# Self-attention softmax of a decoder layer: begun one batch ahead, with row sums and division on VectorE

## The chip, the cores and the metric

One core of a Trainium2 chip runs the whole layer in one launch. The metric is the device time of one execution in microseconds (us), the median of several executions. Engines are called as in the profile: PE (TensorE's matrix products, with PEld for its weight loads), DVE (VectorE), ACT (ScalarE), POOL (GpSimd) and SP, whose queue issues most DMAs.

## The reference, cut to what matters

A decoder layer in fp32 for 16 batches of 112 tokens with 512 features: self-attention with 16 heads of 32, cross-attention to 375 context tokens, and a gated feed-forward block, each behind a layer norm. The change is in the self-attention's softmax:

```python
scores = jnp.einsum('bhqr,bhkr->bhqk', q_r, k_r) * scale     # scale = 1/sqrt(32)
attn = jax.nn.softmax(scores, axis=-1)
y_r = jnp.einsum('bhqk,bhkr->bhqr', attn, v_r)
```

## The kernel before, in words

Tokens are taken in four groups of four batches. For a group, `Group.queries`, `keys` and `values` project the normalised tokens (`xyT`, features on partitions) into `q`, `k` and one `v` per batch. Self-attention then goes batch by batch, by the calls `lay(0)` to `lay(15)` (L1629 to L1672); each call is called a step here.

A step has a fixed order on PE. `scores` (L902) makes, for all 16 heads, 112 x 112 scores with the queries on partitions, in two PSUM tiles of the tag `sc` (two tiles exist, eight heads in each). VectorE takes each row's maximum (L1005) and subtracts it (L1007); ScalarE takes the exponential (L1010) of eight heads in one operation. PE transposes each head's block (L1024) back into the `sc` tiles, so that the keys come onto the partitions, and ScalarE copies that to SBUF as `eT` (L1026). `weighted_values` (L915) multiplies with `v` into the PSUM tile `ys`, and `key_sums` (L930) multiplies the same `eT` with a block of ones, which puts the softmax's row sums into a PSUM bank of the tag `mm`. `Pending` keeps both; its `store`, called in the next step, divides: four reciprocals (L952) and one multiplication (L953) that writes the result into `xyT`.

Between these pieces PE does other work, so that it need not wait. `Filler` holds a queue of such pieces (projections of later groups, products that prepare the feed-forward weight `w2`, transposes of normalised tokens, the output projection `after_self`, first products of cross-attention). A step's second argument `us` says how much of it is to be spread over the step: at least 5.5 us between the scores and the first transposes, further shares after each half's transposes, and `f.drain()` emits what is left at the end. These pieces write into PSUM banks of the tag `mm`, of which three exist; most are emptied by a ScalarE copy (L857, L871, L888, L1538, L827), the output projection by VectorE (L990) and the first cross-attention values by VectorE (L888).

PE's order is the program's order (`manual_schedule`). The other engines' orders are laid out by the framework's planner, which knows estimated costs and takes earlier lines first among what is ready; on the chip each engine then works its queue in that order. `tc.issue_after(x)` puts a block's instructions behind `x` on the engine of `x`. That is used for `pending.store()` and for the preparation of `w2` (`w2_prep`, a generator whose steps are two or three VectorE operations, a ScalarE copy L1567 or some stores by DMA); a step's `prepared` says how many are taken.

SBUF tiles: `pair(name, tag, bufs)` gives a tile for eight heads, and `evp` also holds the cross-attention queries under the tag `q`, which have the same size.

Of the kernel before, what the change touches and what calls it, by code (L numbers as in the profile page):

```python
# [11 lines left out]
F32 = mybir.dt.float32  # L12
I32 = mybir.dt.int32
U8 = mybir.dt.uint8
AF = mybir.ActivationFunctionType
ALU = mybir.AluOpType
AX = mybir.AxisListType

P = 128
B, S, D = 16, 112, 512  # L20
# [3 lines left out]
C = D // P  # L24
H, DH = 16, 32
HG = 4
# [4 lines left out]
GB = 4  # L31
# [4 lines left out]
SCALE = 1.0 / math.sqrt(DH)  # L36
# [548 lines left out]
def mixed(a, b, skip=0):  # L585

    a, b = iter(a), iter(b)
    for _ in range(skip):
        yield next(a)
    while True:  # L590
        took = [next(p, None) for p in (a, b)]
        if took[0] is None and took[1] is None:
            return
        yield sum(t for t in took if t is not None)
# [3 lines left out]
def finite_layer(  # L598
# [30 lines left out]
    nc = tc.nc  # L629
# [12 lines left out]
    def psum(tag, shape, bufs=None):  # L642
        bufs = bufs or banks_of.get(tag, 2)
        return ps[""].tile(shape, F32, tag=tag, bufs=bufs, name=tag)
# [7 lines left out]
    def pair(name, tag="e", bufs=3):  # L652
        return evp.tile([P, 2, HG, S], F32, tag=tag, name=name, bufs=bufs)
# [148 lines left out]
    class Norm:  # L802


        def __init__(self, l, tiles):
            self.l, self.tiles = l, tiles
# [10 lines left out]
        def begin(self):  # L817
            self.start(True)
            yield 0.0
# [18 lines left out]
    def block_products(k):  # L838
        tr = psum("mm", [P, C, P])
        nc.tensor.transpose(tr[:, 0, :], bd[k], ident)  # L840
        nc.scalar.copy(bd[k], tr[:, 0, :])
        nc.tensor.matmul(tr[:, 1, :], bd[0], bd[k], start=True, stop=True)
        nc.scalar.copy(bdm[k], tr[:, 1, :])
        yield 0.5

    def fold(dst, src, block):

        for m in range(C):
            acc = psum("mm", [P, D])
            for j in range(C):  # L850
                if block is None:
                    nc.tensor.transpose(acc[:, ts(j, P)], src[:, j, ts(m, P)], ident)
                else:
                    nc.tensor.matmul(
                        acc[:, ts(j, P)], src[:, j, ts(m, P)], block, start=True, stop=True
                    )
            nc.scalar.copy(dst[:, m, :], acc)  # L857
            yield 0.9
# [43 lines left out]
    def scores(k_of, q_of, rows_):  # L902

        scs = [psum("sc", [P, 2, 512]) for _ in range(2)]
        views = [
            s[:rows_, :, : HG * S].rearrange("p i (j s) -> p i j s", j=HG) for s in scs
        ]
        for j in range(C):
            for i in range(HG):
                nc.tensor.matmul(  # L910
                    views[i // 2][:, i % 2, j, :], k_of(i, j), q_of(i, j), start=True, stop=True
                )
        return views

    def weighted_values(y, v, es, first, last):  # L915


        n = v.shape[0]
        for j in range(C):
            for i in range(HG):  # L920
                nc.tensor.matmul(  # L921
                    y[ts(i, DH), j, :],
                    v[:, HG * j + i, :],
                    es[i // 2][:n, i % 2, j, :],
                    start=first and j == 0,
                    stop=last,
                    skip_group_check=True,
                )

    def key_sums(sums, es, n):  # L930
        for i in range(HG):
            nc.tensor.matmul(  # L932
                sums[ts(i, DH), :, :], ones[:n, :DH], es[i // 2][:n, i % 2], start=True, stop=True
            )

    class Pending:


        def __init__(self):
            self.kept = None  # L940

        def put(self, *kept):
            self.kept = kept

        def store(self):
            if self.kept is None:
                return
            y, sums, b, scale, over = self.kept
            self.kept = None
            r = ln.tile([P, C, S], F32, tag="r", name="r")  # L950
            for c in range(C):
                nc.vector.reciprocal(r[:, c], sums[:, c])  # L952
            nc.vector.scalar_tensor_tensor(  # L953
                xyT[:, :, ts(b, S)], in0=y, scalar=scale, in1=r, op0=ALU.mult, op1=ALU.mult
            )
            if over is not None:
                nc.scalar.activation(
                    r, r, AF.Relu, scale=-1.0, bias=limit[:, 1:], accum_out=over
                )

    pending = Pending()


    class Group:

# [26 lines left out]
            stats(xr[:, t, :], norm.l, t)  # L992
        norm.start(False)

    def self_attention(b, grp, f, us, prepared):
        bl = b % GB
        scs = scores(
            lambda i, j: grp.q[ds(i * DH, DH), j, ts(bl, S)],
            lambda i, j: grp.k[ds(i * DH, DH), j, ts(bl, S)],
            S,  # L1000
        )
        es = []
        for sc in scs:
            mx = ln.tile([S, 2, HG], F32, tag="mx", name="mx")
            nc.vector.reduce_max(mx, sc, axis=AX.X)  # L1005
            e = pair("e", "es", 3)[:S]
            behind = nc.vector.tensor_tensor(  # L1007
                e, sc, mx.unsqueeze(3).to_broadcast([S, 2, HG, S]), ALU.subtract
            )
            nc.scalar.activation(e, e, AF.Exp, scale=SCALE)  # L1010
            es.append(e)
        with tc.issue_after(behind.ins):
            pending.store()
            for _ in range(prepared):
                next(w2_prep, None)
        first = max(0.45 * us, min(us, 5.5))
        f.fill(first)
        eTs = []
        for e, share in zip(es, (0.45 * (us - first), 0.35 * (us - first))):
            tr = psum("sc", [P, 2, 512])  # L1020
            trv = tr[:S, :, : HG * S].rearrange("p i (j s) -> p i j s", j=HG)
            for i in range(2):
                for j in range(C):
                    nc.tensor.transpose(trv[:, i, j, :], e[:, i, j, :], ident[:S, :S])  # L1024
            eT = pair("eT")
            nc.scalar.copy(eT[:S], trv)  # L1026
            eTs.append(eT)
            f.fill(share)
        y = psum("ys", [P, C, S])
        sums = psum("mm", [P, C, S])  # L1030
        weighted_values(y, grp.v[bl][:S], eTs, True, True)
        key_sums(sums, eTs, S)
        pending.put(y, sums, b, 1.0, None)
        f.drain()

# [194 lines left out]
    class Cross:  # L1232
# [6 lines left out]
        def step(self, b, kc, q, keys, f, us):  # L1239
            scs = scores(  # L1240
                lambda i, j: keys.k[ds(i * DH, DH), j, ts(kc, KP)],
                lambda i, j: q[ds(i * DH, DH), j, ts(b % 2, S)],
                KP,
            )
            n = b * KC + kc
            late = self.late

            es = [(pair("es", "es", 3) if kc == 0 else pair("e"))[:KP] for _ in scs]
            self.late = (b, kc, keys.v[kc][:KP], es)
            for i, sc in enumerate(scs):  # L1250
                nc.scalar.activation(  # L1251
                    es[i], sc, AF.Exp, scale=scl[:, n : n + 1], bias=bia[:, n : n + 1]
                )
            for i, sc in enumerate(scs):
                nc.scalar.activation(  # L1255
                    sc,
                    sc,
                    AF.Relu,
                    scale=nscl[:, n : n + 1],
                    bias=limit[:KP, :1],  # L1260
                    accum_out=low[:KP, 2 * n + i : 2 * n + i + 1],
                )
            self.weigh(late)
            for i in range(2):
                self.add(late, i)
            self.divide(late)
            f.fill(us)
# [15 lines left out]
        def divide(self, late):  # L1283
            if late is not None and late[1] == KC - 1:
                sums = psum("mm", [P, C, S])
                key_sums(sums, self.es, KP)

                pending.put(
                    self.y, sums, late[0], 1.0 / (1.0 + 1e-8), top[:, late[0] : late[0] + 1]
                )  # L1290
                pending.store()

# [303 lines left out]
    f = Filler()  # L1598
# [15 lines left out]
    f.drain()  # L1614
    n1[1].start(True)
    f.add(mixed(grp[0].keys(), block_products(1)))
    f.add(mixed(fold(wv, raws[2], bdm[1]), n1[1].transposes()), grp[0].values(range(GB)))
    f.drain()
    w2_load()
# [4 lines left out]

    def lay(b, us, *pieces, prepared=0):
        f.add(*pieces)
        self_attention(b, grp[b // GB], f, us, prepared)

    lay(0, 15.5, mixed(grp[1].queries(), w2_products(h, w2[0])))  # L1629
    lay(1, 15.5, mixed(grp[1].keys(), w2_products(h, w2[1])), prepared=4)  # L1630
# [39 lines left out]
    lay(14, 12, mixed(kv[0].values(), n2[2].transposes(), 3))  # L1670
    qs = [Queries(n) for n in range(B // 2)]
    lay(15, 9.5, qs[0].pieces(), output_bias())  # L1672
    pending.store()

    cross = Cross()
    n3w = None
# [1 line left out]
    for b in range(B):  # L1678
        g, bl = divmod(b, GB)
        us = 0.0  # L1680
# [183 lines left out]
```

## Time and profile before

| | |
|---|---|
| median of three runs | 1392.72 us (1392.26 to 1393.63) |
| profiled execution, its own time | 1394.03 us |
| span of that execution, first to last instruction | 1392.2 us |
| PE busy | 1364.3 us (98%) |
| VectorE, ScalarE, GpSimd busy | 794.7, 428.8, 33.9 us |
| granted TensorE clock | 0.997 |
| steps 0 to 15 of self-attention | 63.4 to 341.6 us |
| cross-attention, then feed-forward | 341.6 to about 853 us, then to the end |

Such lines are read as follows. A group of instructions has its line, engine, operation, the tiles it writes and reads, its shape and count, then total busy time and the mean of one in ns, then the engine's idle time just before it and what ended that. The timeline has start and length in us, the same names, and in brackets the idle time before. A line of waits says which engine and line waited for which, in total, how often, and the longest. fp32 products stand in the trace as two records each. A busy PE is not a PE at its peak, since products are pipelined; costs on PE are therefore better read from start to start.

### The profile page before, as it was taken

Reading aid. Unit: us, or ns where it says so; the run is one execution under the profiler, and the core shown is the slowest. Engines: PE = TensorE matmul, PEld = TensorE weight load, DVE = VectorE, ACT = ScalarE, POOL = GpSimd, SP = SyncE. Lnnn points to the kernel's source line nnn. Section 1 sums busy time; section 2 is a strip of 40 time slices with the busy share of each in tenths; the row PEclk is TensorE's granted clock in tenths of the full one; section 3 lists DMA queues with packets and bytes.
Section 4 is the critical chain, followed back from the end, with each engine's and each line's share of the span. In section 5 each row is a group of like instructions: output and inputs, shape, how many; then the busy total and the mean of one; then the engine's idle time right before and its main releaser. Section 6 shows DMA issues by size and latency. Waiting matters only on the chain.

```text
span 1392.2 us, 20015 instructions
## 1 busy us (share of the span) xinstructions
PE 1364.3 (98%) x8456; PEld 810.2 (58%) x8456; DVE 794.7 (57%) x1477; ACT 428.8 (31%) x677; POOL 33.9 (2%) x68
## 2 busy tenths in 40 slices
PE   8999999999999999999999999999999999999997
PEld 6555555555676667766777775544555555555554
DVE  5146987776555575558454566756754235554332
ACT  3345352324254434443454455110110011111000
POOL 2000010110000100000000000000000000000000
PEclk9999999999999999999999999999999999999999
DMA  9100002601000000000000102111131122312201
GB/s 318 47 1 26 6 16 77 251 7 45 23 23 23 31 23 23 24 23 24 23 23 23 45 12 60 46 46 46 31 123 60 46 64 77 91 61 73 108 0 56
DMA packets 59719, 74.03 MB, mean 53 GB/s; under 512 B 2640, under 2 KB 47712, under 8 KB 57316
## 3 DMA queue, kind: packets, MB, share of 16 engines
q1 hardware_dynamic: 57952, 69.44, 15.1%
q0 software_dynamic: 672, 1.62, 0.4%
q8 instruction: 69, 1.13, 0.3%
q10 hardware_dynamic: 996, 1.59, 0.3%
q14 instruction: 30, 0.25, 0.1%
HBM read 61.63 MB, written 11.01 MB: 52 GB/s over the span
## 4 chain that ended last, share of the span: by engine, by line
PE 88%; DVE 6%; ACT 2%; DMA 1%; issue 1%; POOL 0%; SPq 0%; DVEq 0%; ACTq 0%; POOLq 0%
PE mm L883 14%; PE gate L1450 12%; PE mm L865 9%; PE mm L1103 9%; PE ys L1450 7%; PE mm L894 6%; PE gate L1384 6%; PE mm L1450 5%; PE sc L910 4%; PE ys L1384 3%; PE ys L921 3%; PE mm L1384 3%; PE sc L1024 2%; PE mm L932 2%; PE mm L826 1%
## 5 line engine op out<-in xcount | busy, mean ns | idle before, releaser
L883 PE MATMUL mm<-xv,cT 128*125 128x512 f32 x384 | 179.4, 603 | 3.3 <-DVE v L888 3.3
L1251 ACT ACTIVATE e<-sc,bia,scl 125x896 f32<-125x896 f32 x64 | 68.4, 1094 | 201.0 <-PE sc L910 201.0
L952 DVE RECIPROCAL r<-mm 128x112 f32<-128x112 f32 x128 | 95.5, 808 | 42.5 <-PE mm L932 42.5
L883 PEld LDWEIGHTS mm<-xv,cT 128*125 128x125 f32 x384 | 68.4, 187 | 79.1 <-issue 74.1
L1255 ACT ACTIVATE sc<-sc,limit,nscl 125x896 f32<-125x896 f32 x96 | 102.6, 1068 | 0.0
L1450 PE MATMUL gate<-t,f 128*128 128x448 f32 x256 | 101.4, 539 | 0.0
L1281 DVE TENSOR_TENSOR es<-es,e 125x896 f32<-125x896 f32 x64 | 68.4, 1088 | 47.3 <-ACT e L1251 47.3
L1384 PE MATMUL gate<-h,f 128*128 128x448 f32 x224 | 86.6, 539 | 0.0
L1450 PE MATMUL gate<-xyT,f 128*128 128x448 f32 x192 | 80.1, 540 | 0.0
L1005 DVE TENSOR_REDUCE mx<-sc 112x8 f32<-112x896 f32 x32 | 33.5, 1082 | 77.1 <-PE sc L910 77.1
L1450 PE MATMUL ys<-t,f 128*128 128x448 f32 x192 | 77.4, 539 | 0.0
L1450 PEld LDWEIGHTS gate<-t,f 128*128 128x128 f32 x256 | 48.6, 190 | 47.6 <-issue 47.0
L1103 PEld LDWEIGHTS mm<-kt,xks 128*128 128x128 f32 x360 | 59.0, 190 | 15.3 <-issue 14.6
L1384 PEld LDWEIGHTS gate<-h,f 128*128 128x128 f32 x224 | 42.5, 190 | 41.3 <-issue 40.9
L1466 ACT COPY u<-gate 128x448 f32<-128x448 f32 x16 | 8.5, 531 | 182.3 <-PE gate L1450 109.4
L1103 PE MATMUL mm<-kt,xks 128*128 128x188 f32 x360 | 63.5, 324 | 0.0
L883 PE MATMUL mm<-wv,xyT 128*112 128x512 f32 x128 | 57.8, 596 | 0.3 <-ACT v L888 0.3
L1450 PEld LDWEIGHTS ys<-t,f 128*128 128x128 f32 x192 | 36.5, 190 | 35.7 <-issue 35.5
L865 PE MATMUL mm<-xyT,xq 128*128 128x224 f32 x256 | 52.5, 356 | 4.2 <-ACT xyT L827 4.0
L1396 DVE TENSOR_TENSOR h<-h,h 128x896 f32<-128x896 f32 x32 | 32.8, 1086 | 40.9 <-PE ys L1384 31.6
L1450 PEld LDWEIGHTS gate<-xyT,f 128*128 128x128 f32 x192 | 36.0, 190 | 34.4 <-issue 33.7
L910 PE MATMUL sc<-q,kT 32*125 32x112 f32 x1536 | 54.7, 279 | 0.0
(209 smaller groups left out, 2148.0 us busy)
## 6 DMA issues: line engine op xcount, KB each, us to landing
f<-in_f_w SPq DMA_DIRECT2D x64, 256.0 KB, 3.2
f<-blocks SPq DMA_DIRECT2D x14, 1024.0 KB, 4.8
cT<-in_ctx SPq DMA_DIRECT2D x16, 750.0 KB, 4.7
w<-in_f_w SPq DMA_DIRECT2D x4, 1024.0 KB, 10.5
blocks<-w SPq DMA_DIRECT2D x4, 1024.0 KB, 5.4
xr<-in_x SPq DMA_DIRECT2D x2, 1024.0 KB, 10.7
out_y<-o SPq DMA_DIRECT2D x8, 256.0 KB, 3.2
xr<-in_x SPq DMA_DIRECT2D x2, 768.0 KB, 15.4
```

The lines of the kernel that those rows point to most:

```text
L865: nc.tensor.matmul(acc[:, :n], w[:, c, ts(j, P)], src[:, c, :], start=(c == 0), stop=(c == C - 1))
L883: nc.tensor.matmul(acc[:n, :], src[:, c, :], w[:, c, :], start=(c == 0), stop=(c == C - 1))
L894: nc.tensor.matmul(acc, xyT[:, c, ts(t, P)], w[:, c, :], start=(c == 0), stop=(c == C - 1))
L910: nc.tensor.matmul(views[i // 2][:, i % 2, j, :], k_of(i, j), q_of(i, j), start=True, stop=True)
L921: nc.tensor.matmul(y[ts(i, DH), j, :], v[:, HG * j + i, :], es[i // 2][:n, i % 2, j, :], start=first and j == 0, stop=last, skip_group_che ...
L952: nc.vector.reciprocal(r[:, c], sums[:, c])
L1103: nc.tensor.matmul(acc[:, m], lhs[:, k, ts(m, P)], rhs[:, k], start=first and m == 0 and k == 0, stop=k == 1, skip_group_check=True,)
L1251: nc.scalar.activation(es[i], sc, AF.Exp, scale=scl[:, n : n + 1], bias=bia[:, n : n + 1])
L1255: nc.scalar.activation(sc, sc, AF.Relu, scale=nscl[:, n : n + 1], bias=limit[:KP, :1], accum_out=low[:KP, 2 * n + i : 2 * n + i + 1],)
L1281: nc.vector.tensor_tensor(total, total, late[3][i][:KP], ALU.add)
L1384: nc.tensor.matmul(banks[m][bank], o[:, c, ts(m, P)], t[:, c, :], start=first and c == 0, stop=c == UNITS - 1, skip_group_check=True,)
L1450: nc.tensor.matmul(bank, o[:, s, k, :], t[:, k, :], start=first and k == 0, stop=k == 1, skip_group_check=True,)
```

## The change

`self_attention` becomes a class with two methods. `begin(b)` makes the scores of a batch and the whole softmax: VectorE takes the maxima and multiplies them by -1/sqrt(32); ScalarE takes the exponential straight from PSUM, head by head, with that column as its bias (16 operations of 112 columns for each batch in place of two of 896); VectorE sums the rows, inverts the sums and multiplies. `step(b)` first begins batch b + 1 and then goes on with the transposes of batch b, whose values are divided already. The product with ones goes, and `y` is copied into `xyT` by ScalarE at the end of the same step. The first half's exponentials now lie in a tile of the tag `q`, of which two exist. `begin(0)` comes before step 0, after `grp[0].keys()`, with a `drain` ahead of it. The preparation of `w2` is issued behind the last multiplication of the begun batch, where it was behind the last subtraction. Cross-attention keeps its product with ones and its division, whose lines now stand in `Cross.divide`.

```diff
-    def self_attention(b, grp, f, us, prepared):
...
-        for sc in scs:
-            mx = ln.tile([S, 2, HG], F32, tag="mx", name="mx")
-            nc.vector.reduce_max(mx, sc, axis=AX.X)
-            e = pair("e", "es", 3)[:S]
-            behind = nc.vector.tensor_tensor(
-                e, sc, mx.unsqueeze(3).to_broadcast([S, 2, HG, S]), ALU.subtract
-            )
-            nc.scalar.activation(e, e, AF.Exp, scale=SCALE)
-            es.append(e)
-        with tc.issue_after(behind.ins):
-            pending.store()
...
-        y = psum("ys", [P, C, S])
-        sums = psum("mm", [P, C, S])
-        weighted_values(y, grp.v[bl][:S], eTs, True, True)
-        key_sums(sums, eTs, S)
-        pending.put(y, sums, b, 1.0, None)
+    class SelfAttention:
+        def begin(self, b, grp):
...
+            for sc, (tag, bufs) in zip(scs, (("q", 2), ("es", 3))):
+                mx = ln.tile([S, 2, HG], F32, tag="mx", name="mx")
+                nc.vector.reduce_max(mx, sc, axis=AX.X)
+                nc.vector.tensor_scalar(mx, mx, -SCALE, None, op0=ALU.mult)
+                e = pair("e", tag, bufs)[:S]
+                for i in range(2):
+                    for j in range(HG):
+                        nc.scalar.activation(
+                            e[:, i, j, :],
+                            sc[:, i, j, :],
+                            AF.Exp,
+                            scale=SCALE,
+                            bias=mx[:, i, j : j + 1],
+                        )
+                es.append((e, mx))
+            for e, total in es:
+                nc.vector.reduce_sum(total, e, axis=AX.X)
+                nc.vector.reciprocal(total, total)
+                self.behind = nc.vector.tensor_tensor(
+                    e, e, total.unsqueeze(3).to_broadcast([S, 2, HG, S]), ALU.mult
+                )
+            self.next = b, grp.v, [e for e, _ in es]
+
+        def step(self, b, grp, f, us, prepared):
+            b, v, es = self.next
+            if b + 1 < B:
+                self.begin(b + 1, grp)
+            with tc.issue_after(self.behind.ins):
+                for _ in range(prepared):
+                    next(w2_prep, None)
...
+            y = psum("ys", [P, C, S])
+            weighted_values(y, v[b % GB][:S], eTs, True, True)
+            nc.scalar.copy(xyT[:, :, ts(b, S)], y)
+            f.drain()
...
     f.add(mixed(grp[0].keys(), block_products(1)))
+    f.drain()
+    attention = SelfAttention()
+    attention.begin(0, grp[0])
     f.add(mixed(fold(wv, raws[2], bdm[1]), n1[1].transposes()), grp[0].values(range(GB)))
...
-        self_attention(b, grp[b // GB], f, us, prepared)
+        attention.step(b, grp[min(b + 1, B - 1) // GB], f, us, prepared)
```

More of the change, by code (lines that the diff above doesn't have):

```diff
@@ L934, in key_sums @@
             )
[L936 to L954, printed above, removed]
-            )
[L956 to L961, printed above, removed]
     class Group:
@@ L993, in after_self @@
         norm.start(False)
-    def self_attention(b, grp, f, us, prepared):
[L996 to L1002, printed above, removed]
-        for sc in scs:
-            mx = ln.tile([S, 2, HG], F32, tag="mx", name="mx")
-            nc.vector.reduce_max(mx, sc, axis=AX.X)
-            e = pair("e", "es", 3)[:S]
-            behind = nc.vector.tensor_tensor(
-                e, sc, mx.unsqueeze(3).to_broadcast([S, 2, HG, S]), ALU.subtract
-            )
-            nc.scalar.activation(e, e, AF.Exp, scale=SCALE)
-            es.append(e)
-        with tc.issue_after(behind.ins):
-            pending.store()
[L1014 to L1028, printed above, removed]
-        y = psum("ys", [P, C, S])
-        sums = psum("mm", [P, C, S])
-        weighted_values(y, grp.v[bl][:S], eTs, True, True)
-        key_sums(sums, eTs, S)
-        pending.put(y, sums, b, 1.0, None)
-        f.drain()
@@ new lines, in finite_layer @@
+    class SelfAttention:
+        def begin(self, b, grp):
+            bl = b % GB
+            scs = scores(
+                lambda i, j: grp.q[ds(i * DH, DH), j, ts(bl, S)],
+                lambda i, j: grp.k[ds(i * DH, DH), j, ts(bl, S)],
+                S,
+            )
+            es = []
+            for sc, (tag, bufs) in zip(scs, (("q", 2), ("es", 3))):
[27 more added lines that the diff above has]
+                    next(w2_prep, None)
+            first = max(0.45 * us, min(us, 5.5))
+            f.fill(first)
+            eTs = []
+            for e, share in zip(es, (0.45 * (us - first), 0.35 * (us - first))):
+                tr = psum("sc", [P, 2, 512])
+                trv = tr[:S, :, : HG * S].rearrange("p i (j s) -> p i j s", j=HG)
+                for i in range(2):
+                    for j in range(C):
+                        nc.tensor.transpose(trv[:, i, j, :], e[:, i, j, :], ident[:S, :S])
+                eT = pair("eT")
+                nc.scalar.copy(eT[:S], trv)
+                eTs.append(eT)
+                f.fill(share)
+            y = psum("ys", [P, C, S])
+            weighted_values(y, v[b % GB][:S], eTs, True, True)
+            nc.scalar.copy(xyT[:, :, ts(b, S)], y)
+            f.drain()
@@ L1286, in divide @@
                 key_sums(sums, self.es, KP)
-                pending.put(
-                    self.y, sums, late[0], 1.0 / (1.0 + 1e-8), top[:, late[0] : late[0] + 1]
-                )
-                pending.store()
+                b = late[0]
+                r = ln.tile([P, C, S], F32, tag="r", name="r")
+                for c in range(C):
+                    nc.vector.reciprocal(r[:, c], sums[:, c])
+                nc.vector.scalar_tensor_tensor(
+                    xyT[:, :, ts(b, S)],
+                    in0=self.y,
+                    scalar=1.0 / (1.0 + 1e-8),
+                    in1=r,
+                    op0=ALU.mult,
+                    op1=ALU.mult,
+                )
+                nc.scalar.activation(
+                    r, r, AF.Relu, scale=-1.0, bias=limit[:, 1:], accum_out=top[:, b : b + 1]
+                )
     UNITS = FC // 2
@@ L1672, in finite_layer @@
     lay(15, 9.5, qs[0].pieces(), output_bias())
-    pending.store()
     cross = Cross()
```

## The prediction

> **What bounds the kernel now.** I read the page's busy shares and chain first, then the step windows, the PE waits, and the timeline of single steps. "Step b" is `lay(b)`.
>
> ```profile
> PE 1364.3 (98%) x8456; PEld 810.2 (58%) x8456; DVE 794.7 (57%) x1477; ACT 428.8 (31%) x677; POOL 33.9 (2%) x68
> ...
> PE 88%; DVE 6%; ACT 2%; DMA 1%; issue 1%; POOL 0%; SPq 0%; DVEq 0%; ACTq 0%; POOLq 0%
> ```
>
> TensorE carries the end: any matmul removed is time removed, and every PE wait counts in full, because PE has no idle time in which to catch up. ScalarE and VectorE have room on average; what matters is how late they hand PSUM banks back.
>
> ```profile
> PE sc L1024 <- ACT e L1010: 2.8, 3, 1.4
> PE mm L865 <- ACT kT L871: 0.8, 1, 0.8
> PE ys L921 <- ACT eT L1026: 0.7, 1, 0.7
> ```
>
> These are PE's longest waits in the self-attention steps (63.4 to 341.6 us). Three of 0.3 (two for copies of `v`, one for L953) and 0.4 of "issue" follow: 5.6 us in all. The exponential's 2.8 fall in steps 4 (0.52), 13 (1.39) and 15 (0.90). So little waiting is there to win; the wins must be matmuls. Step 0, in the timeline:
>
> ```profile
> 63.44 1.05 PE L910 MATMUL sc<-kT,qT 32*112 32x112 f32 x32
> ...
> 64.53 2.09 DVE L1005 TENSOR_REDUCE mx<-sc 112x8 f32<-112x896 f32 x2 [27.32 <-PE sc L910]
> 66.03 1.02 PE L1535 MATMUL mm<-w,bd 128*128 128x512 f32 x2
> ...
> 67.09 0.60 ACT L1538 ACTIVATE w<-mm 128x512 f32<-128x512 f32 x1 [2.96 <-PE mm L1535]
> 67.64 0.95 ACT L1010 ACTIVATE e<-e 112x896 f32<-112x896 f32 x1
> ...
> 69.25 1.67 PE L865 MATMUL mm<-xyT,wq 128*128 128x448 f32 x4
> ...
> 71.61 0.93 PE L1024 MATMUL sc<-ident,e 112*112 112x112 f32 x8
> ...
> 80.94 0.93 PE L932 MATMUL mm<-eT,ones 112*32 112x448 f32 x8
> 81.80 1.77 PE L865 MATMUL mm<-xyT,wq 128*128 128x448 f32 x4
> ```
>
> Two things are to be seen: the product with ones holds PE from 80.94 to 81.80; and between scores and first transposes (8.2 us) PE fills three `mm` banks, which ScalarE empties between its two exponentials.
>
> **Removed on PE.** The product with ones costs 81.80 - 80.94 = 0.86 us per step by starts (0.87 in steps 2 and 3); 16 x 0.86 = **-13.8 us**. Its row (15.1 us busy) includes pipelined ends, so I take the starts. No other matmul is added or dropped; scores and transposes keep their number.
>
> **Waits that go.** Step 15 starts no further batch, so its exponential is long done: -0.90. The sums no longer hold an `mm` bank until VectorE's reciprocals in the next step: the 0.82 of step 6 (a third product short of a bank) and the 0.31 of step 12 (behind those reciprocals) go. **-2.0.** The wait for `eT` in step 15 (0.73) and the 0.40 of issue stay.
>
> **ScalarE: the block of exponentials.** Two operations of 0.95 per step become sixteen of 112 columns that read PSUM with a bias per partition. No row shows that size; the nearest are
>
> ```profile
> L873 ACT ACTIVATE q<-mm,bq x32: 429/447/476, 327.7 to 808.6; 128x224 f32<-128x224 f32 x32
> L873 ACT ACTIVATE kT<-mm,bk x4: 556/572/573, 296.3 to 307.0; 128x375 f32<-128x375 f32 x4
> ```
>
> and, from the timeline of step 15,
>
> ```profile
> 333.90 0.77 ACT L873 ACTIVATE q<-mm,bq 128x224 f32<-128x224 f32 x2
> ```
>
> (572 - 447)/151 = 0.83 ns per column, so 447 - 112 x 0.83 = 354 ns at 112. Two in a row took 0.77 where two alone would be 0.89: they overlap by 0.12. Copies at L827 overlap by 0.10. So start to start is 0.23 to 0.25, at the upper end 0.354 if nothing overlaps; I take 0.25, the pessimistic of the two overlaps: 16 x 0.25 + 0.1 = 4.1 us against 1.8. In busy time (+2.3 per step, and 0.53 for the copy of `y`) this is free: the step windows show ScalarE at 8 to 10 of 20 us. What counts is order. ScalarE works its queue in order (in step 4 it idled 1.58 us before 140.94 for a VectorE result while a finished `qT` product waited for its copy until 142.74), and both halves' maxima come within 2.1 us of each other, so all sixteen can run as one block ahead of the copies.
>
> A rule speaks against the change here. The Trainium skill, "ScalarE: Activation LUTs", section "What ACT_TABLE_LOAD costs", gives 280 ns + 0.833 ns per column with a pointer bias and about 93 ns of overlap; the estimate from that page is 0.28 us apiece. No row of this trace shows 112 columns; by 0.28 the whole sum would end at about -2 instead of -6.
>
> **Where the block makes PE wait.**
> - Before step 0: `begin(0)` now sits between `keys` and the folding of `wv`. Scores wait for the last `kT` copy (0.4). PE there makes a bank per 0.67 us on average (0.89 and 0.44 in turn, 44.7 to 49.6) and ScalarE takes about 0.5 for each. Exponentials start 3.5 us after the scores start; three banks cover 2.0 of the 4.1 us, and the first copy needs 0.5. With the 0.4: **+3.0**. Behind it stand only long `values` products, so nothing is given back.
> - Steps 0 and 1: maxima end at 66.53, two scalings (nearest row L774, 0.15 to 0.17) at 66.8, the block runs to 70.95. The `w` bank, ready at 67.05, is emptied at 71.5 if its copy falls behind the block; the product of 69.25 waits 2.3. If the copy goes first, the next bank comes short at 70.75 and waits 1.3. Mean 1.8 each: +3.6.
> - Steps 2 and 3, same working with `values` (1.9 us a half): ends 0.4 and 1.75 in step 2, 0 and 1.9 in step 3; means 1.1 and 1.0, less the 0.6 they wait now: +1.5.
> - Steps 4, 11, 13: the transposes now wait until the block has left the `sc` banks. Maxima are late there already (139.17 in step 4, 262.23 in step 11, about 297.4 in step 13). Step 13: maxima to 299.4, first eight exponentials to 301.7, PE arrives at 300.0: 1.7 against 1.39. Step 4: second half ready 1 us after PE arrives, against 0.52. Step 11: preparation of w2 ends later, 0.8. Together +1.6.
> - Other steps: three products of 3 to 3.5 us fill the 7 to 10 us, the third bank is free: 0.
>
> Added: 3.0 + 3.6 + 1.5 + 1.6 = **+9.7**.
>
> **VectorE.** Out per step: two subtractions (1.0 each), four reciprocals and the multiplication of L953 (3.5): 5.5. In: two scalings (0.2), two row sums and two multiplications (1.0 each, as L1005 and L1007), two reciprocals of 8 columns (between 0.15 of a tiny operation and 0.81 of L952's; 0.2, being tiny): 4.8. Free by size. But row sums wait in queue for the block, about 2.3 us; behind them stand the w2 preparation and, in steps 5, 9, 12 and 14, evictions of `mm`. The third bank covers those (the fourth product starts 9 us after the step); uncovered they would cost up to 1 us each, 4 in all, which goes into the range. The w2 preparation comes some 4 us later in its step. So do its stores and the weight loads behind them in SP's queue, but `xk` was issued at 221 and is used at 293, `xv` at 257 for 309, `xq` at 264 for 326: covered. POOL's memsets and the beta add trail without a user at hand.
>
> **Sum:** -13.8 - 2.0 + 9.7 = **-6.1 us**. The profiled execution took 1394.03 (span 1392.2), 1.3 above the median; it would become 1387.9, the median of 1392.72 about 1386.6. With a little for evictions behind row sums I say 1387.
>
> **Rivals.**
> 1. *Copies slip between the exponentials.* If the order written for ScalarE puts copies ahead of the block or between its halves, nearly all of the 9.7 shrinks to the prologue's smaller half and step 13, about 3: -13.8 - 2.0 + 3 = -12.8, 1380. For it: the order in the trace does mix copies and exponentials (67.09, 67.64, 68.59, 69.02). Against: they mixed because the second exponential was not ready; now both halves are.
> 2. *Slower: the small exponentials do not overlap.* At 0.354 us the block is 5.8 us instead of 4.1, and eight places (prologue, steps 0 to 4, 11, 13) each wait 1.7 longer: +13.3, sum +7.2, 1400. It decides from 0.25 + 6.1/(8 x 16) = 0.30 us per exponential: above that, it is a loss. For it: they read PSUM and a bias column each, as L873 does. Against: two L873 in a row did overlap.
> 3. *Nothing measurable:* the price per exponential near 0.28 to 0.30, or the evictions behind VectorE's row sums taking their 4 us: 1391 to 1394. The change would then trade matmuls for bank waits.
>
> **How the numbers follow.** A measurement here tells about 0.2% (2.8 us) from no change: faster is below 1389.9, slower above 1395.5. The forecast (1382 to 1392) has 0.45, of which 0.09 lies above 1389.9; rival 1 has 0.22; rival 2 0.20; rival 3 0.13, of which 0.02 falls out on either side. Faster 0.36 + 0.22 + 0.02 = 0.60; same 0.09 + 0.09 = 0.18; slower 0.22. The range 1379 to 1397 reaches to rival 1 and leaves out the upper half of rival 2 and a little below.
>
> **What would show it.** PE busy down by 14 to 15 us with L932 left only for the cross stage; exponentials in runs of eight or sixteen with 0.25 us between starts; new PE waits of 1 to 2 us on ScalarE copies of `w`, `qT` and `v` in the first 70 us of steps and about 3 us before step 0; none in step 15 on exponentials; steps 5 to 10 shorter by 0.86 each. I am wrong if step 0 or the prologue shows no bank wait (then rival 1), if starts are over 0.30 apart (rival 2), or if PE waits on VectorE in steps 5, 9, 12 or 14.

## The result, and the profile after

The changed kernel took 1398.18 us (median of five runs, 1395.68 to 1399.85) against 1392.72 for the kernel before: ratio 1.0034, interval 1.0019 to 1.0048. A second measurement of both, side by side, gave 1396.67 against 1393.25: 1.0018 (1.0007 to 1.0029). The change makes this kernel slower, by 0.2 to 0.3%; I had forecast 1387, with 1397 as the upper end. The profiled execution took 1396.93 (span 1395.1, granted clock 0.993), 2.9 us more than that of before.

From the page of the kernel after, the busy times, the shares of the chain that ended last, and the group of the new exponentials (busy time, mean of one in ns, idle time before):

```profile
PE 1357.1 (97%) x8328; PEld 809.2 (58%) x8328; DVE 785.2 (56%) x1493; ACT 470.7 (34%) x917; POOL 36.5 (3%) x68
...
PE 85%; DVE 9%; ACT 4%; issue 1%; DMA 1%; POOL 0%; SPq 0%; ACTq 0%; DVEq 0%; POOLq 0%
...
L986 ACT ACTIVATE e<-sc,mx 112x112 f32<-112x112 f32 x256 | 64.6, 400 | 44.8 <-DVE mx L982 44.7
```

PE lost its 128 records of the product with ones and 7 us of busy time, yet the span grew. The chain shows where to look: its shares of DVE and ACT went from 8% together to 13%. PE's longest waits up to the cross stage (total, how often, longest):

```profile
PE sc L1019 <- ACT e L986: 4.2, 3, 2.6
PE mm L865 <- ACT w L1542: 3.9, 2, 2.0
PE mm L826 <- ACT wv L857: 3.0, 1, 3.0
...
PE mm L883 <- ACT w L1542: 1.5, 1, 1.5
PE mm L1539 <- ACT w L1542: 1.5, 1, 1.5
```

The first row is transposes that wait for exponentials (in steps 4, 10 and 13; steps 4, 11 and 13 were forecast); the `mm` rows are matmuls without a free bank, because the copy that would free it stands behind the block of exponentials. Step 0 in the timeline (start, length, operation, idle time before):

```profile
70.11 2.09 DVE L981 TENSOR_REDUCE mx<-sc 112x8 f32<-112x896 f32 x2 [15.23 <-PE sc L910]
...
71.62 1.02 PE L1539 MATMUL mm<-w,bd 128*128 128x512 f32 x2
...
72.37 4.03 ACT L986 ACTIVATE e<-sc,mx 112x112 f32<-112x112 f32 x16 [2.65 <-DVE mx L982]
...
73.98 1.02 PE L1539 MATMUL mm<-w,bd 128*128 128x512 f32 x2
...
76.18 0.72 ACT L1542 ACTIVATE w<-mm 128x512 f32<-128x512 f32 x1
...
76.94 1.40 PE L865 MATMUL mm<-xyT,wq 128*128 128x448 f32 x3 [1.95 <-ACT w L1542]
```

Sixteen exponentials run from 72.37 to 76.40 as one block. The first `w` product of the step starts at 71.62 and takes 1.02, so its bank is ready at 72.6; its copy stands behind the block and starts at 76.18. PE fills the other two banks until 75.0 and then stands for 1.95 us, until that copy frees the first.

One thing that I had not foreseen is in the windows (stretch, length, busy time and instructions of PE, PEld, DVE, ACT, POOL, then the granted clock, DMA share, GB/s):

```profile
52.50:55.20 2.70, 2.67 (x13) 2.67 (x14) 2.31 (x4) 1.54 (x3) 0.00 (x0) 0.50 0.00 0
...
98.40:104.90 6.50, 6.41 (x18) 3.48 (x19) 4.77 (x8) 2.84 (x6) 0.00 (x0) 0.74 0.01 3
...
308.00:314.00 6.00, 6.00 (x25) 4.43 (x26) 4.63 (x6) 3.79 (x12) 0.26 (x1) 0.73 0.00 0
```

PE's clock was 0.50, 0.74 and 0.73 in these stretches. In the kernel before it was 1.00 in every window from 40 to 345 us, as in this one over its steps:

```profile
63.40:341.60 278.20, 272.43 (x1977) 150.69 (x1976) 202.27 (x328) 112.36 (x166) 17.16 (x20) 1.00 0.15 54
```

Each stretch comes right behind one of the new waits: 3.05 us before 52.53, 1.97 before 98.49, 2.65 before 307.98. While it lasts, a `w` product takes 1.91 us (at 100.56) that takes 1.02 elsewhere, and eight products that fold `wv` take 1.91 (at 53.44) where eight such at 48.43 took 1.06.

The account of the stage, by profile: from the start of what follows the last `kT` product to the first cross-attention scores it was 296.84 us (44.73 to 341.57) and is 299.88 (44.58 to 344.46), 3.04 more.

| | forecast | by profile |
|---|---|---|
| product with ones gone | -13.8 | 16 x -0.75 = -12.0 |
| PE waits, net | +7.7 | 5.65 to 15.6: +9.9 |
| lower granted clock | not priced | 2.7 x 0.50 + 6.5 x 0.26 + 6.0 x 0.27 = +4.7 |
| sum | -6.1 | +2.6 |

The sum leaves 0.4 of the 3.04 open. The account is that of one execution, 2.9 us above the one of before; the medians lie 5.5 and 3.4 us apart in the two measurements, and that remainder is not accounted for step by step. Theory A of the experiments is this account (the block of exponentials delays the copies that free banks, and some waits cost clock besides); the rivals stand in the expectations.

### The profile page after: what moved, and what is told of

It reads as the page before. It is cut to its first block, busy times and chain, and to the rows that moved or that the text cites. A ratio compares the mean times of both kernels' runs of the same rounds, so it can differ in the third digit from the quotient of the medians.

```text
span 1395.1 us, 20037 instructions
## 1 busy us (share of the span) xinstructions
PE 1357.1 (97%) x8328; PEld 809.2 (58%) x8328; DVE 785.2 (56%) x1493; ACT 470.7 (34%) x917; POOL 36.5 (3%) x68
## 4 chain that ended last, share of the span: by engine, by line
PE 85%; DVE 9%; ACT 4%; issue 1%; DMA 1%; POOL 0%; SPq 0%; ACTq 0%; DVEq 0%; POOLq 0%
PE mm L883 13%; PE gate L1454 12%; PE mm L1096 9%; PE mm L865 8%; PE ys L1454 7%; PE mm L894 6%; PE gate L1388 6%; PE mm L1454 5%; PE sc L910 4%; PE ys L1388 3%; PE ys L921 3%; PE mm L1388 3%; ACT e L986 2%; DVE mx L981 1%; PE sc L1019 1%
## 5 line engine op out<-in xcount | busy, mean ns | idle before, releaser
L986 ACT ACTIVATE e<-sc,mx 112x112 f32<-112x112 f32 x256 | 64.6, 400 | 44.8 <-DVE mx L982 44.7
L1284 DVE RECIPROCAL r<-mm 128x112 f32<-128x112 f32 x64 | 47.9, 810 | 39.8 <-PE mm L932 39.8
```

The costliest lines, as they stand in the source:

```text
L986: nc.scalar.activation(e[:, i, j, :], sc[:, i, j, :], AF.Exp, scale=SCALE, bias=mx[:, i, j : j + 1],)
```

## The experiments

**Prologue block moved.** `begin(0)` after the folding of `wv` and the transposes, just ahead of the long `values` products.

```diff
-    f.add(mixed(fold(wv, raws[2], bdm[1]), n1[1].transposes()), grp[0].values(range(GB)))
+    f.add(grp[0].values(range(GB)))
# and ahead of the drain before attention.begin(0, grp[0]):
+    f.add(mixed(fold(wv, raws[2], bdm[1]), n1[1].transposes()))
```

> The changed kernel with one move: begin(0) stands behind the folding of wv and the token transposes, ahead of the long values products. Theory A (the block of sixteen exponentials holds back the copies that free PSUM banks, and PE waits of 2 us and more also cost clock for some us afterwards): the 3.05 and 0.28 us of waits ahead of step 0 go, and with them the 2.7 us stretch at half clock (1.35): 1398.2 - 4.7 = 1393.5. Theory B (waits cost only their own length): 1398.2 - 3.3 = 1394.9. Theory C (VectorE's row sums are the cause): no change, 1398.

Measured: 1392.23 (1388.60 to 1394.80) against 1393.66, ratio 0.9991 (0.9981 to 1.0000), which is 3.8 to 6.0 us better than the change itself, by its two ratios. The 3.05 and the half-clock stretch behind it are gone; the other waits stand as they were (1.93, 1.95, 1.52, 1.52, 1.27, 2.63). So does the 0.28 that the expectation puts ahead of step 0: it stands in step 7 of the change (at 196.21). The time lies under both figures expected (1393.5 and 1394.9), so it does not tell by itself whether the clock has a share. The profile says more: the stage is 4.9 us shorter (44.75 to 339.69), of which 3.2 are waits. Half clock is left only behind step 13, for 6.8 us where it was 3.4; behind the 1.95 of step 1 there is none now. That is 1.5 us less clock lost.

**Subtraction instead of bias.** Everything else of the change is kept, the early start, the division ahead of the transposes and the missing product among it.

```diff
-                nc.vector.tensor_scalar(mx, mx, -SCALE, None, op0=ALU.mult)
...
-                for i in range(2):
-                    for j in range(HG):
-                        nc.scalar.activation(e[:, i, j, :], sc[:, i, j, :], AF.Exp, scale=SCALE, bias=mx[:, i, j : j + 1])
+                nc.vector.tensor_tensor(
+                    e, sc, mx.unsqueeze(3).to_broadcast([S, 2, HG, S]), ALU.subtract
+                )
+                nc.scalar.activation(e, e, AF.Exp, scale=SCALE)
```

> The changed kernel with the maximum subtracted by VectorE as before and one exponential of 896 columns per half in place of eight with a bias; still begun a batch ahead, row sums and division still on VectorE. Theory A: the ScalarE block shrinks from 4.0 to 1.8 us in two pieces, so the waits ahead of step 0 (3.3) and in steps 0 to 3 (7.0) fall to about 0.6 and most of the 4.7 us of lost clock goes: about 1385. Theory B: 1398.2 - 9.7 = 1388.5. Theory C: VectorE works 1.7 us more per step, so 1398 or slower.

Measured: 1383.75 (1381.60 to 1386.85), ratio 0.9930 (0.9917 to 0.9942). This is the verdict on the bias: in its place it costs 12.3 to 14.5 us (1.0018 or 1.0034 less 0.9930, of 1393). No wait for a bank is left in steps 0 to 3. What the subtraction costs is seen further on, in PE's waits from 100 to 345 us:

```profile
PE mm L826 <- DVE xn L792: 2.5, 1, 2.5
PE sc L1013 <- DVE e L983: 2.0, 1, 2.0
```

VectorE, with 1.8 us more per step (2.1 of subtractions in place of 0.3 of scaling), is now late where it also prepares `w2` and the next group's tokens.

**PE kept busy in its waits.** Matmuls of the identity with itself, whose result nobody reads, are put at the places where PE waits: 12 before step 0; 8, 8, 6 and 6 in steps 0 to 3; 5 and 11 in steps 4 and 13. Nothing else is changed.

```diff
+    def busy(n):
+        t = psum("ys", [P, C, P])
+        for k in range(n):
+            nc.tensor.matmul(t[:, k % C, :], ident, ident, start=True, stop=True)
```

> The changed kernel with products of the unit matrix by itself, never read, put on PE just where it waits (12 ahead of the third token transpose, 8 in steps 0 and 1, 6 in steps 2 and 3, 5 and 11 ahead of the transposes of steps 4 and 13; about 0.22 us each, so a little less than each wait). Theory A: PE stays at full clock, the three stretches at 0.50, 0.74 and 0.73 of the clock go, about -4.5: 1393.7. Theory B: the clock has nothing to do with the waits, or costs nothing: 1398 or above.

Measured: 1391.66 (1390.45 to 1392.93), ratio 0.9985 (0.9976 to 0.9994): with 56 more matmuls it is 4.6 to 6.8 us faster than the change. The windows of this kernel over the same three places:

```profile
52.00:56.00 4.00, 3.65 (x21) 2.39 (x20) 3.10 (x4) 2.80 (x7) 0.00 (x0) 1.00 0.07 22
94.00:104.00 10.00, 9.83 (x43) 5.92 (x43) 8.62 (x13) 8.00 (x22) 0.00 (x0) 1.00 0.00 0
300.00:312.00 12.00, 11.81 (x103) 8.61 (x105) 7.84 (x11) 7.45 (x22) 5.42 (x7) 1.00 0.00 1
```

The clock column reads 1.00 in all three, where the change had stretches of 0.50 to 0.74, and the stage takes 295.28 us (44.87 to 340.15) instead of 299.88: 4.6 us, beside the 4.7 of the account. The banks still come when ScalarE frees them; what is bought back is the clock behind the waits. This settles that term: with no clock loss to recover, more matmuls could not have made the kernel faster.

**The block split in the steps.** The second half's exponentials, the row sums and the divisions are written behind the step's first filling; the prologue keeps its block whole.

```diff
             first = max(0.45 * us, min(us, 5.5))
             f.fill(first)
+            if b + 1 < B:
+                self.finish()    # second half's exponentials, both row sums and divisions
```

> The changed kernel with the second half's eight exponentials, the row sums and the multiplications written behind the step's first filling, so that copies of ready banks come between the halves; ahead of step 0 the block stays whole. Theory A: the waits of steps 0 to 3 (7.0 us) fall under 1 and the stretch at 0.74 of the clock in step 1 goes (1.7): about 1390. Rival: ScalarE has too much to do in these steps whatever its order (11 of 20 us): within 1 us of 1398.

Measured: 1389.62 (1387.92 to 1392.27), ratio 0.9976 (0.9967 to 0.9984), 5.9 to 8.1 us better than the change. ScalarE's order in step 0 becomes eight exponentials, copies of `w` and `qT`, then the rest, and no bank wait is left in steps 0 to 3 (7.0 us before); the 3.04 before step 0 and 2.64 of step 13 stay, and 2.06 of step 4 take the place of 1.28. Its longest waits up to the cross stage:

```profile
PE sc L1029 <- ACT e L993: 5.3, 4, 2.6
PE mm L826 <- ACT wv L857: 3.0, 1, 3.0
```

The stage is 5.8 us shorter (44.85 to 338.92), with 6.2 less of waits; half clock shows in three places as in the change, with one now behind step 4 instead of step 1, so nothing was won on the clock. The exponentials are the same in number and price, and VectorE's sums and divisions come later, not earlier: it is their order on ScalarE, ahead of the copies, that cost the time.

**Both together**: late `begin(0)` and split block, still with the bias.

> The changed kernel with its bias per head on ScalarE kept for all batches, and the moves of e1_late_begin and e4_split_block together. Theory A: the bank waits ahead of step 0 and those of steps 0 to 3 are separate places, so their gains add: 1398.2 - (1398.2 - 1392.2) - (1398.2 - 1389.6) = 1383.6. Rival: both hang on one resource (ScalarE's total time), so the second gives little: 1389.

Measured: 1384.92 (1384.34 to 1386.29) against 1393.25, ratio 0.9938 (0.9926 to 0.9951). The two add up. What is left are 1.90 in step 4, 2.65 in step 13 and four waits under 0.8.

**The product with ones kept**, unread, in the kernel with the subtraction.

```diff
             weighted_values(y, v[b % GB][:S], eTs, True, True)
+            key_sums(psum("mm", [P, C, S]), eTs, S)
```

> The kernel of e2_subtract (1383.8) with the product with ones put back behind the weighted values, its sums never read. This prices the removed product by itself. The prediction's 0.86 per step: +13.8, 1397.5. By the starts in the changed kernel (ys to the next product 0.91 us, where with the product it was 1.66): 0.75 x 16 = +12.0, 1395.8. Rival: ScalarE and VectorE bound these steps and the product was hidden: under +5.

Measured: 1389.87 (1388.97 to 1391.66) against 1392.74, ratio 0.9979 (0.9970 to 0.9988): 6.8 us more by the ratios, half of what was expected. By starts the product does hold PE as reckoned: step 0 to step 1 takes 20.07 us with it (65.59 to 85.66) and 19.31 without (66.07 to 85.38), 0.76 a step. But the wait of 2.46 for `xn` goes, and 1.30 and 1.96 become 0.60 and 0.50: PE now arrives later at VectorE's results. These are 4.6 us; three small waits go too, 1.2 in all, and 1.2 of new waits for `eT` stand against them. So 16 x 0.76 less 4.6 is 7.6, and 0.8 of difference to the 6.8 stays unassigned.

**The bias alone**, in the kernel before: per-head exponentials, and nothing else of the change.

```diff
-            behind = nc.vector.tensor_tensor(
-                e, sc, mx.unsqueeze(3).to_broadcast([S, 2, HG, S]), ALU.subtract
-            )
-            nc.scalar.activation(e, e, AF.Exp, scale=SCALE)
+            behind = nc.vector.tensor_scalar(mx, mx, -SCALE, None, op0=ALU.mult)
+            # 16 activations per batch with bias, as in the change
```

> The kernel before with only the maximum made a ScalarE bias per head (sixteen exponentials of 112 columns in each step); product with ones, division and same-step order as before. Theory A: bank waits of 1.5 to 2 us in steps 0 to 3, more in 1 to 3 because the sums hold a bank, the transposes wait in steps 4 and 13, and clock is lost: +10 to +14 on 1393.7, so 1404 to 1408. Rival: it takes 2 us of VectorE work off each step's chain, so a small gain: 1390.

Measured: 1415.45 (1411.61 to 1417.86), ratio 1.0159 (1.0143 to 1.0175): 22 us, well over what I expected. PE's waits from 60 to 364 us:

```profile
PE mm L865 <- DVE r L952: 10.3, 3, 4.2
PE mm L1541 <- DVE r L952: 3.2, 3, 1.4
```

The row sums hold one of three `mm` banks until VectorE's reciprocals, so the block meets two free banks: 13.5 us of PE's waits end with a reciprocal, of 20.9 in all, where the kernel before waits 5.6 over its steps. The change has no such bank to wait for, which fits that the same block costs less there; no run frees that bank alone.

**No batch ahead.** The kernel with the subtraction, but each batch is begun in its own step, so division and transposes follow directly.

```diff
         def step(self, b, grp, f, us, prepared):
+            self.begin(b, grp)
             b, v, es = self.next
-            if b + 1 < B:
-                self.begin(b + 1, grp)
```

> The kernel of e2_subtract (1383.8) with each batch begun in its own step, so the transposes wait for maximum, subtraction, exponential, row sum and multiplication of the same batch: about 8 us to the first half, 9.5 to the second, against arrivals of PE at 8 and 10 to 13 us. Theory A: PE waits where the maxima are late (steps 4, 6, 13: some 2 us more each) and in the short steps 3, 5, 12 (up to 1 each): +8 and some clock, 1392 to 1394. Rival: the start a batch ahead gives nothing: 1384.

Measured: 1422.75 (1419.51 to 1424.02), ratio 1.0202 (1.0189 to 1.0216). The direction was right, the size missed by far. PE's waits up to 400 us:

```profile
PE sc L1012 <- DVE e L993: 19.1, 5, 6.3
PE sc L1012 <- DVE mx L992: 14.0, 8, 4.8
```

The transposes wait 33 us for divisions and sums, and the windows show a clock of 0.83 to 0.94 behind many of these waits. In step 4 the first half's maximum starts at 137.87 and its division ends only at 147.2: VectorE's queue takes the preparation of `w2` between the links of the chain. The early start hides this.

**Subtraction early, bias later.** Late `begin(0)`; batches up to 5 are subtracted by VectorE (where banks are short), later ones use the bias (where VectorE is short).

> The changed kernel with begin(0) behind the folding, and with the subtraction on VectorE and whole exponentials for the batches begun up to step 4 (b up to 5), heads with a bias on ScalarE after that. Theory A: no bank waits before step 5; VectorE, lighter by 1.7 us a step from step 5 on, brings the tokens of step 6 in time (2.5 + 0.6 + 1.3 us of waits in e2_subtract go); step 13 waits 2.6 instead of 2.0: about 1380. Rival: nothing beyond e2_subtract, 1384.

Measured: 1382.78 (1382.63 to 1383.31), ratio 0.9925 (0.9912 to 0.9939), clearly better than both the kernel before and the change; from subtraction throughout it can't be told. Its clock read 1.00 throughout the steps, and its only PE wait over 1 us there is one of 2.64 for exponentials (three such waits, 3.8 us in all).

**Scores later in two steps.** The same, but in steps 4 and 13 the next batch is begun behind the transposes, to take away that 3.8.

```diff
-            if b + 1 < B:
+            behind_transposes = b in (4, 13)
+            if not behind_transposes:
                 begin()
...
+            if behind_transposes:
+                begin()
```

> The kernel of e7_mixed (1382.8) with one more move: in steps 4 and 13, where the maxima come late, the next batch is begun behind the transposes instead of ahead of them, so that no transpose waits for an sc bank that the exponentials still hold. Theory A: the waits of 2.64 (step 13) and 0.92 (about step 4) go and with them what clock they cost: -3.6 to -5, 1378 to 1379. Rival: the waits only move to the following step, whose transposes then find their e unfinished: 1382 to 1384.

Measured: 1393.89 (1393.23 to 1395.27), ratio 1.0006 (0.9997 to 1.0015); both expectations were wrong. PE in the timeline:

```profile
152.19 0.45 PE L910 MATMUL sc<-kT,qT 32*112 32x112 f32 x4 [2.37 <-DVE e L984]
...
308.84 0.72 PE L910 MATMUL sc<-kT,qT 32*112 32x112 f32 x4 [3.45 <-ACT e L993]
```

The next step's scores now come soon after the late ones and find the `sc` banks still held; the transposes of step 5 wait 2.93 for exponentials besides. The waits did not go but moved and grew, by 7 us, and the clock in the windows of 20 us from 140 (0.91) and from 300 (0.83) adds 20 x 0.09 + 20 x 0.17 = 5.2. Together 12, where the span grew by 10.9.

**The change again**, beside the last two on their chip.

> The changed kernel itself once more, beside the others: 1395.5 to 1400 if its scatter over runs is that of its first measurement, with the granted clock lowest in the longest runs (theory A: whether a wait of about 2 us costs clock differs from run to run).

It gave the second ratio above, and its profile has the same waits and half clock behind the same three. Over the 17 timed executions of the change, time follows the granted clock: 1392.1 to 1395.7 where the mean clock was 0.996 or 0.997, 1396.6 to 1399.9 where it was 0.991 to 0.995. The same program loses a varying amount to the clock.

## Why the prediction was wrong, step by step

*Product with ones, -13.8.* Right in kind, 15% too large. Step 0 before the change (first line; the product with ones and what follows it, at 80.94 and 81.80, stand in the prediction) and after it (the other two):

```profile
80.14 0.97 PE L921 MATMUL ys<-eT,v 112*32 112x112 f32 x32
...
87.94 0.97 PE L921 MATMUL ys<-eT,v 112*32 112x112 f32 x32
88.85 1.77 PE L865 MATMUL mm<-xyT,wq 128*128 128x448 f32 x4
```

The next work starts 0.91 us after the value product starts, where before the change 1.66 passed (80.14 to 81.80): 0.75, not 0.86. I read from the start of the product to be removed, and forgot that the value product ahead of it, no longer overlapped by it, shows 0.91 itself instead of 0.80.

*Waits that go, -2.0.* The waits of steps 6, 12 and 15 did go; so did the 0.40 of issue, which was to stay.

*Price of one exponential.* 4.03 us for sixteen against 4.1 forecast, 0.25 from start to start. One lasts 400 ns against the 354 that I extrapolated, and a larger overlap makes up for it, which was luck. By the estimate of 0.28 from the Trainium skill ("ScalarE: Activation LUTs", "What ACT_TABLE_LOAD costs") sixteen would take 4.5 us; here the measured 0.25 decides. Rival 2, no overlap, is refuted.

*Waits added, +9.7.* The mechanism held in all places but step 11: before step 0 3.05 (3.0 forecast, 0.4 of it for a `kT` copy that the scores did not wait for), steps 0 and 1 1.95 and 1.97 (1.8 each), steps 2 and 3 1.53 each (1.1 and 1.0), step 4 1.28 (1.0), step 13 2.65 (1.7), step 11 none (0.8). In steps 0 to 3 I averaged over two orders of copies where the block came first each time; in steps 0 and 1 that order was forecast at 2.3 and took 1.95, so the mean came out close by luck, in steps 2 and 3 it did not; in step 13 the maxima end only at 305.45, and the transposes start at 307.98, after the first eight exponentials. Three waits of 0.2 to 0.4 in steps 7 and 10 were not forecast. With the waits that go this is +9.9 net against +7.7. Rival 1 (copies slip between) did not happen by itself; made to happen in the split kernel, it gave its gain.

*The step that failed: a wait on PE costs its length.* "Every PE wait counts in full", says the prediction; three of them counted for more. I priced every wait at its duration and put the clock at nothing, without a reason. The waits brought 4.7 us of slower matmuls in the profiled execution, and filling them with useless ones gave 4.6 to 6.8 back. Without this term the forecast's error would have been half as large: -12.0 + 9.9 = -2.1 instead of +2.6, still short of what a measurement tells from no change. With the clock kept at 1.00 the changed kernel took 1391.66, inside the range.

The Trainium skill, "TensorE: Matmul & The Clock Gate", section "Why this matters for your kernels", asks for no PE-idle gaps over about 3 us. By that rule only the 3.05 would have been at risk. The runs disagree: clock was lost behind waits of 1.97 and 2.65 (here), 1.95 (the bias alone, at 71.67) and 2.06 (step 4 of the split kernel); none behind 1.95 in step 0 here, nor behind any of 1.53, nor behind 2.46 with the subtraction or 2.64 in the mixed kernel.

Why the same length sometimes costs and sometimes not can be read from shorter windows. In the change half clock begins at 51.83, 99.62 and 307.83 and lasts 3.41 us each time; these starts are 14 and 61 times 3.413 us apart. In every run with more than one such stretch the starts lie on a grid of 3.413 us, at a place of its own in each execution, and up to the cross stage a stretch lasts 3.41 or 6.83. What seems to count is how much of a wait falls into one cell of that grid. Two cells of the change, the first with most of the wait of step 0, the second with all of that of step 1, and the cell behind the second:

```profile
75.73:79.14 3.41, 2.19 (x6) 1.19 (x7) 3.31 (x5) 2.08 (x6) 0.00 (x0) 1.00 0.00 0
96.21:99.62 3.41, 1.44 (x4) 0.68 (x4) 3.31 (x5) 3.15 (x11) 0.00 (x0) 1.00 0.00 0
99.62:103.03 3.41, 3.41 (x9) 1.64 (x8) 3.38 (x6) 0.52 (x1) 0.00 (x0) 0.50 0.00 0
```

PE stood for 1.21 us of the first cell and 1.97 of the second, and only the second was followed by half clock. From 40 us to the cross stage, 23 of the 24 stretches in all runs begin behind a cell with 1.90 us or more of waits; one begins behind 1.47 (the late scores, at 154.7), and two cells with 1.92 and 1.95 (late scores and mixed kernel) had none behind them. This is read off afterwards; no run moved a wait within the grid to test it.

*VectorE.* Nothing waited for its evictions in steps 5, 9, 12 or 14, so the 4 us in the range were not needed.

Of the miss of 8.7 us in the profiled execution (-6.1 to +2.6), 4.7 is the clock, 2.2 the waits, 1.8 the product.

## What to carry to other kernels

A change that takes work off PE where it bounds the kernel, but makes it wait, can pay twice for the waits: their length, and slower matmuls for some microseconds behind some of those of about 2 us or more. Sixteen small operations written as one block ahead of the copies that free PSUM banks stall the engine that fills the banks, however idle ScalarE is on average; split the block, or start it where long products follow. Before moving work from a loaded engine to an idle one, count the free banks over the length of the longest block in its queue.

## What the runs showed of the hardware

The granted clock halves for 3.41 us (sometimes 6.83) behind some PE waits of 1.9 us and more, at starts that lie on a grid of 3.413 us within an execution; in the change, matmuls whose result nobody reads, put into the waits, kept it at 1.00. Exponentials of 112 columns from PSUM with a bias per partition last 400 ns each and follow each other every 0.25 us. The product with ones, four tiles of 32 columns, cost PE 0.75 to 0.76 us per step, although its records add up to 15.1 us in 16 steps, 0.94 each.
